# Layer 2's product from rows that are not yet normalized, and its end one half of the rows at a time beside layer 3's first sums

## Chip, core and metric

The kernel runs on one core of one Trainium2 chip. The metric is the time of one execution in device microseconds: the median of three runs of the kernel before is 1959.56 us (1958.17 to 1960.24). Durations below come from one profiled execution. The engines are PE (TensorE, with PEld for its weight loads), DVE (VectorE), ACT (ScalarE), POOL (GpSimd) and SP (SyncE, which issues most of the transfers).

## What is computed

Four graph layers run one after the other over N = 2708 nodes of D = 128 features with a weighted adjacency matrix of 2708 x 2708 (f32). After each layer its result is added to x and x is normalized over its features:

```python
x = _layernorm(x + layer0(x, adj, ...))   # layers 0 to 3 alike
# layer 0: messages gelu(s_i + d_j + b), weighted by adj, summed; update; gelu; + x; layernorm
# layer 1: messages = x @ W_msg + b; gates = sigmoid(q @ k.T / scale + bias) * adj * adj
#          relu([x, gates @ messages] @ W_upd + b); layernorm
# layer 2 (hyperbolic, curvature 1):
x = proj(x)
h = proj(mobius_matvec(W, x))             # tanh(|xW| / |x| * artanh|x|) * xW / |xW|
h = proj(mobius_add(h, proj(expmap0(b))))
local = logmap(h_i, h_j); att = sigmoid(scores) * adj
support = einsum('ij,ijd->id', att, local)
h = proj(expmap(support, h)); h = relu(logmap0(h)); return proj(expmap0(h))
# layer 3:
x1 = swish((adj @ x) @ W + b); x2 = swish((adj @ x1) @ W + b)
```

## The kernel before

The rows of x are 22 tiles of 128 (the last has 20 rows), in SBUF as x[128, 22, 128]. `runs()` (L190) splits them into two halves of 11 tiles, `groups()` into groups of four tiles. The compiler's scheduler orders the instructions, except inside `tc.manual_schedule()`, where they keep the order in which the program issues them. On each engine the instructions run in one fixed order. Transfers that SP issues go through its queue in that order.

*normalize* (L199) works out, from batch-norm statistics of 11 tiles, a scale r and an offset for each row: some ten short DVE operations and a Sqrt on ACT (L219). Then it applies them tile by tile, even tiles on DVE (L230), odd ones on ACT (L228).

*Resnorm* (L232) closes layers 0 and 1. `add` normalizes the layer's own output h, multiplies it by gamma, adds it to x and takes x's statistics (L238 to L243). `end` normalizes x. `all` does add for early rows, add for late rows, end for early, end for late. In layer 0, which is the function with the pair blocks, `U.norm.add(*early)` stands ahead of the last two groups' sums and rows (L885 to L893); a count `bad_n` of rows that the fast path can't handle follows (L896 to L907). Where it is above zero, the whole is computed again by other code, which didn't run here.

*Layer 1* (L976) first makes, group by group: four transposes of x, xT (copied by ACT, L1020), the message product mT (L1022, L1023), qT (L1026) and the rows of messages and updates (L1031, L1032), with w_both and b_both put together on POOL from four copies (L1000 and following). Then comes its loop over 22 adjacency tiles with the gates, in which `weights2` (L302 onward) makes layer 2's small weights step by step, one step per tile. It ends with `norm.all()`.

*Layer 2* starts with `transposed(xT, x)` (L1169, L259, L261), the products M = x W with three more columns (L1176, copied by ACT, L1177), statistics of M (L1179), and a long chain of 22-column operations to X. Then it transposes `prod[0]` and `prod[1]`, ten columns for each row tile, into `aux[0]` and `aux[1]`, and a score column into slB (L1250 to L1258). The pairs loop follows, up to about 1623 us.

*Layer 2's end* (`end(hf)`, L1443) takes one half of the rows through nine stages that are separated by `yield`: transposes of VT (L1475) into u and of V0T into V0; product and row sums (L1486, L1466); `each` (L1457), 11 instructions of one tile; squares on ACT (L1462); norms, tanh, artanh on 11 columns; `each` into x and its statistics (L1524, L1525); `normalize` (L1527). A loop (L1529 to L1536) lets the two halves take turns, stage by stage. Ahead of it SP loads VT0 and the first ten adjacency tiles, 1354 KB each, into `held`.

*Layer 3* (L1542) sums twice over the 22 tiles: `neighbours` issues for each tile six products of up to 512 columns (L1604, two passes each) into six PSUM banks, in a hand-written order of held (h) and streamed (f) tiles; three buffers stream the others. The last 3 (first pass) or 6 (second pass) tiles are taken bank by bank, and each bank's swish follows. All of this stands in a section of its own, whose pools open when layer 2's end has closed its own.

Of the kernel before, what the change touches and what calls it, by code (L numbers as in the profile page):

```python
# [39 lines left out]
def gnn_stack(ctx: ExitStack, tc: tile.TileContext, t, out: bass.AP):  # L40
# [32 lines left out]


    x = keep.tile([P, NT, D], F32, name="x")
    xsq = keep.tile([P, NT], F32, name="xsq")
# [24 lines left out]
    class Values:  # L101


        def __init__(self, pool, tag):
            self.pool, self.tag, self.n = pool, tag, 0
# [92 lines left out]

    def normalize(dst, src, st, a, b, V, sq=None):  # L199

# [20 lines left out]
        r = V.recip(V.add(root, V.mul(w, V.recip(root))))  # L221
        off = stt(both, -0.5, r, ALU.mult, ALU.mult)
        if sq is not None:
            nc.vector.scalar_tensor_tensor(sq[:, a:b], var, 4.0 * D, V.mul(r, r), op0=ALU.mult, op1=ALU.mult)
        for i in range(a, b):
            c = slice(i - a, i - a + 1)
            if i % 2:
                nc.scalar.activation(dst[:, i, :], src[:, i, :], AF.Identity, bias=off[:, c], scale=r[:, c])  # L228
            else:
                nc.vector.tensor_scalar(dst[:, i, :], src[:, i, :], r[:, c], off[:, c], op0=ALU.mult, op1=ALU.add)  # L230

    class Resnorm:  # L232


        def __init__(self, h, xb, g, st, st2, V, sq=None):
            self.h, self.xb, self.g, self.st, self.st2, self.V, self.sq = h, xb, g, st, st2, V, sq

        def add(self, a, b):  # L238
            h = self.h
            normalize(h, h, self.st, a, b, self.V)  # L240
            nc.vector.tensor_tensor(h[:, a:b, :], h[:, a:b, :], over_tiles(self.g, b - a), op=ALU.mult)
            nc.vector.tensor_tensor(x[:, a:b, :], self.xb[:, a:b, :], h[:, a:b, :], op=ALU.add)
            moments(self.st2, x, a, b)  # L243

        def end(self, a, b):
            normalize(x, x, self.st2, a, b, self.V, self.sq)

        def all(self):
            for a, b in runs():
                self.add(a, b)  # L250
            for a, b in runs():
                self.end(a, b)
# [49 lines left out]
    def weights2(pool, bank):  # L302
# [41 lines left out]
        nc.vector.tensor_copy(w2[:, D:], ps[:, :3])  # L344

# [31 lines left out]
    with ExitStack() as l0:  # L377
# [10 lines left out]
        with ExitStack() as msg:  # L388
# [449 lines left out]
            with tc.manual_schedule():  # L838
# [46 lines left out]
                early, late = runs()  # L885
                U.norm.add(*early)
                for n in range(ahead, G):
                    U.sums(n)
                for n in range(ahead, G):
                    U.rows(n)  # L890
                U.norm.add(*late)
                U.norm.end(*early)
                U.norm.end(*late)  # L893

# [10 lines left out]
                ps = p_misc.tile([P, BANK // P, P], F32, name="ps")  # L905
                nc.tensor.matmul(ps[:1, 0, :1], ones, most, start=True, stop=True)
                nc.vector.tensor_copy(bad_n, ps[:1, 0, :1])  # L907
# [68 lines left out]
    def layers_1_to_3(top, before_end=lambda: None):  # L976

        with ExitStack() as l1:
# [9 lines left out]
            w_both = wp.tile([P, 2 * D], F32, name="w_both")  # L988
            b_both = wp.tile([P, 2 * D], F32, name="b_both")
            xb = wp.tile([P, NT, D], F32, name="xb")  # L990
            w_msg, w_q, w_k = weight("L1_gnn_W_msg"), weight("L1_gnn_W_q"), weight("L1_gnn_W_k")
            upd_x, upd_a = weight("L1_gnn_W_upd", 0), weight("L1_gnn_W_upd", P)
            msg_bc, msg_br = column("L1_gnn_b_msg"), across("L1_gnn_b_msg")
            gate_b = across("L1_gnn_gate_bias")
            upd_b, gamma, beta = across("L1_gnn_b_upd"), across("L1_gnn_ln_gamma"), across("L1_gnn_ln_beta")

            with ExitStack() as pre:
                psum = pre.enter_context(tc.tile_pool(name="ps_pre1", bufs=2, space=PSUM))
                nc.gpsimd.memset(both[:, NT - 1, :], 0.0)
                for k, (w, b) in enumerate(((w_msg, msg_br), (upd_x, upd_b))):  # L1000
                    nc.gpsimd.tensor_copy(w_both[:, k * D:(k + 1) * D], w)
                    nc.gpsimd.tensor_copy(b_both[:, k * D:(k + 1) * D], b)
# [36 lines left out]
            with ExitStack() as att:  # L1039
# [8 lines left out]
                norm = Resnorm(h, xb, gamma, st, st2, Values(rp, "v1_"), xsq)  # L1048
# [40 lines left out]
                with tc.manual_schedule():  # L1089
# [25 lines left out]
                    norm.all()  # L1115
# [10 lines left out]
        with ExitStack() as l2:  # L1126
# [27 lines left out]
            with ExitStack() as pre:  # L1154
# [7 lines left out]
                prod = [pp.tile([P, NT, KP], F32, name=f"prod{k}") for k in range(2)]  # L1162
                part = [pp.tile([P, NT], BF16, name=f"part{q}") for q in range(3)]
                for k in range(2):
                    nc.gpsimd.memset(prod[k], 1.0)
# [28 lines left out]
                th = W.act(W.mul(W.mul(nM, s0), ax), AF.Tanh)  # L1194
# [55 lines left out]
                jobs = [(aux[k], KP, lambda i, r, k=k: prod[k][:r, i, :]) for k in range(2)]  # L1250
                jobs.append((slB, P, lambda i, r: sl[:r, i:i + 1].to_broadcast([r, P])))
                for dst, m, src in jobs:
                    for n, (a, b, r) in enumerate(groups()):
                        ps = psum.tile([P, BANK], F32, name="ps")
                        for i in range(a, b):
                            nc.tensor.transpose(ps[:m, (i - a) * P:(i - a) * P + r], src(i, r), ident[:r, :r])
                        w = (b - a - 1) * P + r
                        (nc.scalar.copy if n % 2 else nc.vector.tensor_copy)(dst[:, a * P:a * P + w], ps[:m, :w])  # L1258
# [162 lines left out]
        HELD = min(NT, 10)  # L1421
        held = top.enter_context(tc.tile_pool(name="adj3", bufs=1))
        kept = {}
# [4 lines left out]
        with ExitStack() as fin:  # L1428
            fp = fin.enter_context(tc.tile_pool(name="fin2", bufs=1))
            tp = fin.enter_context(tc.tile_pool(name="fin2t", bufs=2))  # L1430
            psum = fin.enter_context(tc.tile_pool(name="ps_fin2", bufs=6, space=PSUM))
            VT0 = fp.tile([P, HW], F32, name="VT0")
            nc.sync.dma_start(out=VT0, in_=v_tab)
            for j in range(HELD):
                kept[j] = held.tile([P, N], F32, name=f"held{j}")
                nc.sync.dma_start(out=kept[j], in_=adjT[j * P:(j + 1) * P, :])
            u = fp.tile([P, NT, D], F32, name="u")
            sv = fp.tile([P, NT, D], F32, name="sv")
            st = fp.tile([P, NT, 6], F32, name="st")
            nc.gpsimd.memset(u[:, NT - 1, :], 0.0)  # L1440
            nc.gpsimd.memset(V0, 0.0)

            def end(hf):  # L1443
                a, b = ((0, HT), (HT, NT))[hf]
                n = b - a
                V = Values(fp, f"v2{hf}_")
# [4 lines left out]
                def temp():  # L1451
                    return tp.tile([P, max(HT, NT - HT), D], F32, name="tmp")[:, :n, :]
# [36 lines left out]
                q = squares(uh)  # L1489
                yield  # L1490
# [38 lines left out]
            with tc.manual_schedule():  # L1529
                ends = [end(1), end(0)]  # L1530
                while ends:
                    for e in list(ends):
                        try:
                            next(e)
                        except StopIteration:
                            ends.remove(e)  # L1536
        xs.close()

        with ExitStack() as l3:  # L1542
            wp = l3.enter_context(tc.tile_pool(name="l3", bufs=1))
            STREAM = 3
            stream = l3.enter_context(tc.tile_pool(name="adj3s", bufs=STREAM))
            turns = l3.enter_context(tc.tile_pool(name="turns3", bufs=3))
            pacc = l3.enter_context(tc.tile_pool(name="ps_acc3", bufs=1, space=PSUM))
            psum = l3.enter_context(tc.tile_pool(name="ps_l3", bufs=2, space=PSUM))
            w3, b3 = weight("L3_gnn_W"), across("L3_gnn_b")
            V = Values(wp, "v3_")  # L1550
            nT = wp.tile([P, N], F32, name="nT")
            x1 = wp.tile([P, NT, D], F32, name="x1")
            st = wp.tile([P, NT, 6], F32, name="st")
            nc.vector.memset(x1[:, NT - 1, :], 0.0)
            banks = spans(0, N, BANK)

            def in_turns(pattern, near_by, far):

                near_by, far = list(near_by), list(far)
                order = [(near_by if c == "h" else far).pop(0) for c in pattern]  # L1560
                return order + near_by + far
# [27 lines left out]
            def neighbours(src, order, have, at_end, then, meanwhile=None):  # L1589
# [5 lines left out]
                def tile_of(j):  # L1595
                    at = have.get(j)
                    if at is None:
                        at = last[j] = stream.tile([P, N], F32, name="at")
                        nc.sync.dma_start(out=at[:rows[j], :], in_=adjT[j * P:j * P + rows[j], :])
                    return at  # L1600
# [6 lines left out]
                for j in order[:-at_end]:  # L1607
# [3 lines left out]
                    if meanwhile is not None and j == order[0]:  # L1611
                        meanwhile()
# [14 lines left out]
            def finish(a, b, r, g, gate):  # L1627
# [6 lines left out]
                normalize(x, x, st, a, b, V)  # L1634
# [7 lines left out]
            far = list(range(HELD, NT))[::-1]  # L1642
            near_by = list(range(HELD))
            last = {}
            with tc.manual_schedule():
                order = in_turns("hhfhfhfhfhffhffhfffhhf", near_by, far)
                first = neighbours(x, order, kept, 3, keep)
                back = far[::-1]
                have, last = kept | {j: last[j] for j in back[:STREAM]}, {}
                order = back[:STREAM] + in_turns("hfhfhfhffhfhhhhhfff", near_by, back[STREAM:])  # L1650

# [41 lines left out]
```

## Time and profile before

| what | us |
|---|---|
| median of three runs | 1959.56 |
| the profiled execution | 1961.88 |
| its span | 1960.2 |
| PE busy | 1662.2 (85%) |
| DVE busy | 1549.8 (79%) |
| ACT busy | 1119.8 (57%) |
| POOL busy | 676.7 (35%) |
| PE busy, 880 to 930 (layer 0's end) | 9.65 of 50 |
| PE busy, 960 to 1215 (layer 1's loop and end) | 222.11 of 255 |
| PE busy, 1631 to 1716 (layer 2's end) | 2.35 of 85 |
| PE busy, 1714 to 1822 (layer 3's first sums) | 107.96 of 108 |
| PE busy, 1822 to 1940 (layer 3's second sums) | 110.59 of 118 |

The page gives each engine's busy time, and then the span in 40 equal slices of 49 us, with one digit for the busy tenths of each. A group line has the source line, engine, operation, output and inputs with shapes and a count; then busy time and the mean of one in ns; then the idle time of the engine just before such an instruction and what ended most of it. A timeline line has start, duration, engine, line and operation, and in brackets the idle time before it and its releaser.

### The profile page before, as it was taken

To read this page: it belongs to the slowest core of one execution; us is meant where nothing else is said; L and a number is where in the kernel's file an instruction comes from. 1 tells how busy PE (TensorE), PEld (TensorE's weight loads), DVE (VectorE), ACT (ScalarE), POOL (GpSimd) and SP (SyncE) were. 2 spreads that over 40 slices of the span, in tenths; PEclk is the share of its full clock that TensorE was granted. 3 is DMA by queue.
4 is the path that set the end of the run, shared out by engine and by line. 5 is a ranking of instruction groups with operands and counts; after the bars stand their busy time and mean duration, and the time that the engine had idled before them with its cause. 6 is when DMAs were issued, how large, how long until landed. Compare 5 with 4: busy or idle time off the path is not lost.

```text
span 1960.2 us, 36493 instructions
## 1 busy us (share of the span) xinstructions
PE 1662.2 (85%) x13993; PEld 952.3 (49%) x13993; DVE 1549.8 (79%) x3657; ACT 1119.8 (57%) x1551; POOL 676.7 (35%) x431
## 2 busy tenths in 40 slices
PE   5999999999999999881999992889999972099995
PEld 5666666666666666661544442322223321044542
DVE  7899999999999999868588858699999997800104
ACT  3666676676666667553344434799989973300103
POOL 5667667767767767571100000020000440000000
PEclk8899999999999999995999996889989986589997
DMA  8756667667667666440344401122222207044320
GB/s 216 162 117 146 132 129 147 127 132 149 126 132 151 121 136 141 80 88 5 131 157 159 155 3 59 45 87 87 75 69 95 97 2 298 0 160 156 135 96 30
DMA packets 218695, 222.25 MB, mean 113 GB/s; under 512 B 28373, under 2 KB 204859, under 8 KB 212051
## 3 DMA queue, kind: packets, MB, share of 16 engines
q1 hardware_dynamic: 167470, 196.15, 32.8%
q0 software_dynamic: 51040, 23.68, 10.3%
q8 instruction: 111, 1.82, 0.4%
q14 instruction: 74, 0.60, 0.1%
HBM read 211.94 MB, written 7.83 MB: 112 GB/s over the span
## 4 chain that ended last, share of the span: by engine, by line
DVE 41%; PE 31%; POOL 9%; issue 7%; DMA 6%; ACT 6%; SPq 0%; DVEq 0%; ACTq 0%; POOLq 0%
PE acc L1604 10%; POOL far L739 8%; PE lg L1063 5%; PE acc L1070 5%; DVE ix L735 5%; DMA far<-d_tab,ix 3%; DVE W L840 3%; DVE u L1322 3%; DVE w L1336 3%; DVE m L1325 3%; DVE extra L753 2%; DVE o L697 2%; DVE m L1339 2%; DVE m L1342 2%; PE sl L775 2%
## 5 line engine op out<-in xcount | busy, mean ns | idle before, releaser
L739 POOL DMA_INDIRECT far<-d_tab,ix x352 | 561.7, 1596 | 260.1 <-DVE W L840 112.6
L853 ACT ACTIVATE g<-sl 128x768 f32<-128x768 f32 x484 | 393.4, 813 | 258.0 <-PE sl L780 201.9
L775 PE MATMUL sl<-dA,S 124*128 124x153 f16 x4840 | 408.9, 232 | 10.3 <-DVE W L840 7.8
L775 PEld LDWEIGHTS <-S 124*128 124x128 f16 x4840 | 331.1, 98 | 80.1 <-issue 68.4
L791 PE MATMUL acc<-g,W 128*32 128x128 f32 x4840 | 206.1, 278 | 0.5 <-DVE W L840 0.5
L1296 POOL TENSOR_TENSOR at<-at,off 128x128 f32<-128x128 f32 (+1 forms) x22 | 68.3, 3120 | 339.9 <-DVE m L1325 171.7
L791 PEld LDWEIGHTS acc<-g,W 128*32 128x32 f32 x4840 | 140.9, 109 | 58.8 <-issue 54.8
L1604 PE MATMUL acc<-held,x 128*128 128x512 f32 (+1 forms) x240 | 99.3, 562 | 82.6 <-ACT x L228 82.6
L780 PE MATMUL sl<-s,same 50*128 50x384 f16 x968 | 162.0, 308 | 0.0
L280 DVE TENSOR_TENSOR g<-ps,row_L_gnn_b 128x512 f32<-128x512 f32 (+2 forms) x14 | 7.9, 574 | 191.5 <-PE ps L278 191.5
L840 DVE TENSOR_TENSOR W<-sl,own 128x150 f32<-128x150 f32 x484 | 143.2, 300 | 14.9 <-ACT g L853 14.7
L1352 PE MATMUL accV<-m,X 128*128 128x512 f32 (+4 forms) x264 | 130.5, 637 | 27.4 <-DVE m L1342 26.5
L1304 PE MATMUL ps<-XT 128*128 128x512 f32 (+4 forms) x264 | 142.4, 622 | 6.4 <-DVE m L1307 3.3
L1064 ACT ACTIVATE w<-lg,row_L_gnn_gate_bias 128x512 f32<-128x512 f32 (+1 forms) x132 | 83.5, 636 | 106.1 <-PE lg L1063 104.8
L665 DVE TENSOR_SCALAR S<-rk 124x1000 f16<-124x1000 bf16 (+1 forms) x330 | 133.2, 429 | 0.0
L735 DVE FIND_INDEX8 ix<-v,o 128x8 uint32<-128x2728 f32 x44 | 131.7, 2994 | 0.0
L1063 PE MATMUL lg<-qT,mT 128*128 128x512 f32 (+2 forms) x264 | 121.2, 547 | 3.6 <-ACT w L1064 3.1
L1070 PE MATMUL acc<-w,both 128*128 128x512 f32 (+2 forms) x264 | 121.2, 547 | 0.0
L753 DVE SCALAR_TENSOR_TENSOR extra<-far,v,extra 128x128 f32<-128x128 f32 x330 | 114.9, 348 | 6.3
L1604 PE MATMUL acc<-at,x 128*128 128x512 f32 (+3 forms) x288 | 118.4, 559 | 0.0
L697 DVE SCALAR_TENSOR_TENSOR o<-ps,ar 128x496 f32<-128x496 f32 x132 | 82.5, 625 | 37.5 <-issue 22.6
L1604 PEld LDWEIGHTS acc<-held,x 128*128 128x128 f32 x240 | 45.0, 196 | 134.8 <-ACT x L228 82.9
(315 smaller groups left out, 2634.8 us busy)
## 6 DMA issues: line engine op xcount, KB each, us to landing
at<-in_adjT SPq DMA_DIRECT2D x40, 1354.0 KB
ar<-in_adj SPq DMA_DIRECT2D x105, 248.0 KB
far<-s_tab SPq DMA_DIRECT2D x44, 512.0 KB
at<-in_adjT SPq DMA_DIRECT2D x42, 448.0 KB
at<-in_adjT SPq DMA_DIRECT2D x21, 704.0 KB
at<-in_adjT SPq DMA_DIRECT2D x21, 650.0 KB
held<-in_adjT SPq DMA_DIRECT2D x10, 1354.0 KB
at<-in_adjT SPq DMA_DIRECT2D x21, 280.0 KB
```

The costliest lines, as they stand in the source:

```text
L735: nc.vector.max_index(ix, self.v[:, n * 8:n * 8 + 8], self.o.rearrange("p b j -> p (b j)"))
L739: nc.gpsimd.indirect_dma_start(out=self.far[n][:, k, :], out_offset=None, in_=d_tab[:, :], in_offset=bass.IndirectOffsetOnAxis(ap=self.ix[ ...
L753: nc.vector.scalar_tensor_tensor(self.extra, f, w, self.extra, op0=ALU.mult, op1=ALU.add)
L775: nc.tensor.matmul(group[c], self.S[h][:, n, c, :], dA[q][:, b, c, :], start=c % 3 == 0 and q == 0, stop=False)
L780: nc.tensor.matmul(out, same[p], self.s3[p, :e - a, :], start=False, stop=True)
L791: nc.tensor.matmul(self.acc[q:q + 32, k, :], W[:, c, :], g[:, c, :], start=b == 0 and k == 0, stop=ends)
L840: nc.vector.tensor_tensor(W[:, :, :RG].rearrange("p (k c) i -> p k c i", k=2), columns_of(sl, D, DA), own[:, None, None, :].to_broadcast([ ...
L853: nc.scalar.activation(g.rearrange("p (k c) d -> p k c d", k=2), columns_of(sl, 0, D), AF.Gelu, scale=1.0 / D_SCALE)
L1063: nc.tensor.matmul(lg, mT[:, j * P:j * P + r], qT[:, a:b], start=True, stop=True)
L1070: nc.tensor.matmul(acc[k], mrow[:rows[j], j, :], ws[j][:rows[j], a:b], start=j == 0, stop=j == NT - 1)
L1304: nc.tensor.matmul(ps, XT[:, self.js], XT[:, c], start=True, stop=False)
L1604: nc.tensor.matmul(acc[k], src[:rows[j], j, :], at[:rows[j], a:b], start=j == order[0], stop=j == order[-1])
```

## The change

1. `normalize` is split into `normalizer` (statistics to scale and offset) and `shift` (apply them, with a string that says which engine takes which tile). `Resnorm.begin` is the first half of the old `add`, with all shifts on ACT; `add` goes in groups of four tiles.
2. Layer 0: the count of bad rows first, then early rows begun and added, the last two groups' sums and rows between, late rows begun, early rows ended with all shifts on DVE, late rows added and ended.
3. Layer 1: w_both and b_both are loaded side by side. Its end is `all_but_end`: both halves begun, both added, and one normalizer over 22 columns gives scale xr, offset xo and xsq. x itself stays unnormalized.
4. Layer 2's product takes these rows with W's columns centred (one more step in `weights2`), and xr enters the norm of x. Its end applies the shift to x, a half at a time, on ACT between two of its stages.
5. The two aux sets are transposed together, 42 columns, and copied by ACT (first) and DVE (second).
6. Layer 2's end and layer 3 share one section. Half 1 goes through `end` completely, then half 0. Layer 3's first pass takes half 1's 11 tiles first (21, 11, 20, 12, 19, 13, 18, 14, 17, 15, 16), then half 0's (0, 10, 9, 2, 8, 7, 3, 6, 5, 1, 4). Held are tiles 11 to 15, 0 and 1. Tiles 2 and 3 are loaded into X's space and into the space of VT0 and the temporaries, when half 0's end has used them. The PSUM pool for the transposes has two buffers (six before), the pool for the swish two (three before).

```diff
+    def shift(dst, src, a, b, by, turns="va"):
+        r, off = by
         for i in range(a, b):
             c = slice(i - a, i - a + 1)
-            if i % 2:
+            if turns[i % len(turns)] == "a":
                 nc.scalar.activation(dst[:, i, :], src[:, i, :], AF.Identity, bias=off[:, c], scale=r[:, c])
             else:
                 nc.vector.tensor_scalar(dst[:, i, :], src[:, i, :], r[:, c], off[:, c], op0=ALU.mult, op1=ALU.add)
...
+        def begin(self, a, b):
+            shift(self.h, self.h, a, b, normalizer(self.st, a, b, self.V), "a")
         def add(self, a, b):
-            h = self.h
-            normalize(h, h, self.st, a, b, self.V)
-            nc.vector.tensor_tensor(h[:, a:b, :], h[:, a:b, :], over_tiles(self.g, b - a), op=ALU.mult)
-            nc.vector.tensor_tensor(x[:, a:b, :], self.xb[:, a:b, :], h[:, a:b, :], op=ALU.add)
-            moments(self.st2, x, a, b)
+            for k, m in spans(a, b, 4):
+                h = self.h[:, k:m, :]
+                nc.vector.tensor_tensor(h, h, over_tiles(self.g, m - k), op=ALU.mult)
+                nc.vector.tensor_tensor(x[:, k:m, :], self.xb[:, k:m, :], h, op=ALU.add)
+                moments(self.st2, x, k, m)
+        def end(self, a, b, turns="va"):
+            shift(x, x, a, b, normalizer(self.st2, a, b, self.V), turns)
+        def all(self, between=lambda: None):
+            early, late = runs()
+            self.begin(*early)
+            self.add(*early)
+            between()
+            self.begin(*late)
+            self.end(*early, "v")
+            self.add(*late)
+            self.end(*late)
+        def all_but_end(self):
+            for a, b in runs():
+                self.begin(a, b)
+            for a, b in runs():
+                self.add(a, b)
+            normalizer(self.st2, 0, NT, self.V, xsq, (xr, xo))
...
         nc.vector.tensor_copy(w2[:, D:], ps[:, :3])
+        yield
+        ps = bank()
+        nc.vector.tensor_scalar(w_rows, ident, -1.0 / D, None, op0=ALU.add)
+        nc.tensor.matmul(ps[:, :D + 3], w_rows, w2, start=True, stop=True)
+        nc.vector.tensor_copy(w2, ps[:, :D + 3])
...
-                th = W.act(W.mul(W.mul(nM, s0), ax), AF.Tanh)
+                th = W.act(W.mul(W.mul(nM, W.mul(s0, xr)), ax), AF.Tanh)
...
+                for n, c, ps in turned(lambda i, r: prods[:r, i, :], 32 + KP):
+                    nc.scalar.copy(aux[0][:, c], ps[:KP])
+                    nc.vector.tensor_copy(aux[1][:, c], ps[32:32 + KP])
...
+        HELD, STREAM = 7, 3
+        near1 = list(range(HT, HT + 5))
+        near0 = list(range(HELD - len(near1)))
+        spare0 = list(range(len(near0), len(near0) + 2))
+        far1 = [j for j in range(HT, NT) if j not in near1][::-1]
+        far0 = list(range(spare0[-1] + 1, HT))[::-1]
...
+            x1, nT = u, sv.rearrange("p n d -> p (n d)")[:, :N]
...
                 q = squares(uh)
+                shift(x, x, a, b, (xr[:, own], xo[:, own]), "a")
                 yield
...
-                ends = [end(1), end(0)]
-                while ends:
-                    for e in list(ends):
-                        try:
-                            next(e)
-                        except StopIteration:
-                            ends.remove(e)
...
+                ends = [end(1), end(0)]
+                for e in ends:
+                    next(e)
+                for e in ends:
+                    for _ in e:
+                        pass
+                def more():
+                    for j, at in spare.items():
+                        kept[j] = fetch(j, at)
+                order = (in_turns("fhfhfhfhfhf", h=near1, f=far1)
+                         + in_turns("hffsffsffhf", h=near0, f=far0, s=spare0))
+                first = neighbours(x, order, kept, 3, keep, more, len(far1 + near1) - 1)
+                back = (far1 + far0)[::-1]
                 have, last = kept | {j: last[j] for j in back[:STREAM]}, {}
-                order = back[:STREAM] + in_turns("hfhfhfhffhfhhhhhfff", near_by, back[STREAM:])
+                order = back[:STREAM] + in_turns("hfhfhfhffhffhhhhfff", h=kept, f=back[STREAM:])
```

## The prediction, before the result was known

> **What bounds the kernel now.** I read first the page's slices, then the windows around the one long hole in TensorE's row, the waits and the timeline there, and last the two smaller holes.
>
> ```profile
> PE   5999999999999999881999992889999972099995
> ...
> L1604 PE MATMUL acc<-held,x 128*128 128x512 f32 (+1 forms) x240 | 99.3, 562 | 82.6 <-ACT x L228 82.6
> ```
>
> PE is full nearly everywhere, so time can be won only in the slices that read 0 to 2: slice 35 (about 1666 to 1715 us), slice 19 (about 880 to 930) and slice 25 (about 1176 to 1225). The largest is before layer 3's first sums (L1604): a single wait of 82.6 us for a normalized x.
>
> ```profile
> 1631.00:1656.00 25.00, 0.39 (x4) 0.15 (x2) 22.28 (x67) 9.42 (x12) 0.00 (x0) 0.61 1.00 425
> 1656.00:1716.00 60.00, 1.96 (x3) 0.96 (x4) 52.27 (x221) 22.01 (x31) 0.00 (x0) 0.50 0.05 22
> 1740.00:1800.00 60.00, 60.00 (x159) 28.37 (x159) 0.00 (x0) 0.00 (x0) 0.00 (x0) 1.00 0.48 171
> ```
>
> Columns: window, length, busy PE, PEld, DVE, ACT, POOL, PE clock, DMA share, GB/s. While PE stands still, DVE is busy 74.6 of 85 us with the two halves of layer 2's end, turn by turn. Once layer 3 runs, PE is busy 60.00 of 60 us and DVE 0.00. So DVE's 85 us and PE's first sums lie one after the other, though each half of x feeds half of the tiles. By 1656 the adjacency tiles are in SBUF: DMA isn't the limit.
>
> ```profile
> 1635.43 2.98 DVE L1457 SCALAR_TENSOR_TENSOR u<-X,v,u 128x128 f32<-128x128 f32 x11
> 1646.58 1.28 ACT L145 ACT_TABLE_LOAD   x1
> 1709.75 2.42 ACT L228 ACTIVATE x<-x,v,v 128x128 f32<-128x128 f32 x6 [1.17 <-DVE v L205]
> 1738.11 4.71 PE L1604 MATMUL acc<-at,x 128*128 128x512 f32 x12
> ```
>
> These are the prices: 2.98 us for 11 row tiles on DVE, 1.28 for a table, 0.40 a tile for ACT's shift, and about 4.71 us a tile on PE (12 instructions, two passes for each of six banks).
>
> **What the Trainium skill says.** "TensorE: Matmul & The Clock Gate", What you observe: matmuls run at about half speed until some 4 us of sustained activity. The trace agrees: from 1714.04 the products are 0.85 us apart, after 1718.3 0.43. "ScalarE: Activation LUTs", What ACT_TABLE_LOAD costs: 1283 ns, and about 1380 ns of drain more. The trace has 1.28 us, but the Sqrt begins 0.02 us after the load (1646.58 + 1.28, then 1647.88), so I charge 1.3 and no drain. "DMA: Bandwidth & Descriptors", Where 436 GB/s comes from: the ports end at about 435; here 425.
>
> **Part 1, layer 2's end half by half.** Both halves' transposes stay first, with two PSUM buffers instead of six: each of the eight groups may wait for its copy (4 tiles, about 0.5 us on ACT). Zero to 3 us; I take 0.9. Then half 1 goes alone through the chain that in the trace both shared. Step by step, from 1631.65, the end of V0's copies:
> - product and sum 1.62 + 1.62, small steps 0.5, eleven tiles 2.98: u at 1638.4; square 1.38 on ACT: 1639.9.
> - New here: normalizing x, left out of layer 1, stands on ACT between the square and the Sqrt. Eleven shifts at 0.39: 4.35, to 1644.25. Table 1.3, Sqrt 0.2: 1645.75. In the meantime DVE's sum (1.62) is done, so about 3.9 of the 4.35 lie on this half's chain.
> - reciprocal and products to the tanh 1647.3; eleven tiles 1650.6; square and sum 1653.7; small steps 0.95; eleven tiles 1657.6; two squares on ACT 1660.5; second sum 1662.4; Sqrt 1663.1, small steps 1664.1.
> - artanh and tanh, in the trace 1684.68 to 1689.85: 5.2, to 1669.2; tanh, reciprocals 1.3: 1670.5; eleven tiles 1673.5; statistics 2.15: 1675.7.
> - normalizer 2.07 (1707.68 to 1709.75): 1677.75; six shifts on ACT 2.42: 1680.2.
>
> With 0.9 for the transposes PE can start at about 1681.1 instead of 1714.04: a gain of 33. In the new order tile 21 comes first, and its x is the last of those six shifts, so no earlier start is possible. Half 1 has 11 tiles at 4.71 = 51.8 and about 3 for the slow clock at the start, as now: to about 1736. Half 0 begins on DVE at about 1679 (DVE's queue has it behind half 1) and needs the same 48: ready at about 1727, 9 us before PE asks. So it is hidden entirely, and the rest of layer 3 keeps its length and moves by 33. If that cover went, each us of half 0 beyond 9 would cost one us.
>
> What is moved and queued: SP fetches seven held and three streamed tiles (ten, as now), then tile 2 into X and tile 3 into the room of VT0 and the temporaries. These two wait on DVE's last use, about 1705 and 1711, and the remaining seven are queued behind them. The first of those is asked for at about 1741, 30 us later, and a tile takes 3.3 us at 425 GB/s: no wait. The second pass streams ten tiles instead of nine; before its last group of six tiles the last fetch has one tile and some of the next (about 8 us) to land in instead of about 12: 0, at worst 2. Range of the part: 26 (transposes 3, stages 2, a second slow clock 2) to 36 (shift half hidden, no PSUM wait, fewer small gaps).
>
> **Part 2, layer 1's end and layer 2's product.** Before, layer 1's additions end at 1196.7; then both halves are normalized, transposed and multiplied, and the statistics of M end at 1212.63.
>
> ```profile
> 1192.88 1.62 DVE L242 TENSOR_TENSOR x<-xb,both 128x1408 f32<-128x1408 f32 x1
> 1208.87 3.76 DVE L1179 BATCH_NORM_STATS2 st<-M 128x6 f32<-128x128 f32 x19
> 1236.46 4.23 PE L1256 MATMUL ps<-ident,prod 128*10 128x128 f32 x22 [0.71 <-DVE prod L1237]
> ```
>
> After: late rows' Sqrt waits on ACT behind eleven early shifts (1179.1 to 1183.5), and DVE waits for it until 1183.7, with all additions queued behind. Then 1.1, then six groups: mult, add and statistics of four tiles 2.25, of three 1.8, in all 12.6: 1197.4, no gain so far. But transposes and products of the earlier groups run beside that. Left on DVE after 1197.4: memset 0.91 and mask 0.22, one normalizer of 22 columns about 2.6, four xT copies at 0.69 = 2.8, 22 statistics at 0.2 = 4.4: 10.7, to 1208.1. Gain 4.5; the extra product with the rows' scale is 0.2. Bounds 2 (PE or the copies of M late) and 7 (copies before the additions end).
>
> The aux transposes: 44 of ten columns in 7.45 us (1236.46 to 1243.9) become 22 of 42. One set takes about 0.19 x 22 = 4.2, but each group is copied twice (ACT 0.57, then DVE 0.68, three buffers), so about 4.5 to 5.5 instead of 7.45, and the vector that slB needs is not held up by DVE's copies. Gain 3 (1 to 5). Together 7.5, bounds 3 and 12. Centring W is one tensor_scalar, one matmul of 128x131 and one copy, a further step inside layer 1's loop: 0.3 + 0.4 + 0.4 on engines that are busy there 206 (DVE) and 222 (PE) of 255 us, about 0.7 lost, 0 to 1.5.
>
> **Part 3, layer 0's end.** Before: early additions end 909.3, late 921.5, early rows normalized 925.1, late 929.6; then layer 1's first transposes, and PE needs about 4.3 us for each group of four tiles; the third group's message product starts at 943.46. After: early shifts on ACT alone (11 x 0.39) with additions in groups, to about 910.5; sums 5 and 6 and late statistics to 915.7; late shifts 4.3 on ACT, early rows' Sqrt behind them: 920.2. DVE's eleven early shifts 3.0: 924.4, so PE gets the first tiles at about 922.5 instead of 931.5. But two groups only. Late additions (6.3) lie on DVE between layer 1's copies (six, 4.1): to about 935; their Sqrt is on ACT behind the first two groups' work, and late rows are there from about 938.4; 2 us for transposes and copy, and the third group's product starts at 940.5 to 941. Gain 2.5, bounds 0 (late rows as late as 941.5) and 6 (PE never waits). The bias and weight copies on POOL that fall away lay beside DVE: 0.
>
> **Sum.** 33 + 7.5 - 0.7 + 2.5 = 42.3. The profiled execution took 1961.88 with a span of 1960.2; it becomes 1919.6 with a span of 1917.9. The median of the runs shown is 1959.56, 2.3 below: 1917.3.
>
> **Rivals.**
> - **The chain for half 1 is longer than I add up** (two PSUM buffers, DVE alone exposing each hand-over to ACT that the other half now fills): PE at about 1694, gain 20 instead of 33, 29.3 in all: 1930. For it: the waits list DVE for ACT only 5.3 us in six times, because the halves fill each other's gaps; against it: I took the steps from unshared stretches. Half 0 would be longer too, and past 9 us PE would wait a second time.
> - **More is won** (both front stages near their upper bounds, 12 and 6, and 36 in the end): 54, 1905.6. For it: PE starts sooner after its last work in three places.
> - **No overlap, slower:** the first product waits for the later end as well. Two ends one after the other put PE's start at 1680.2 + 0.9 + 47.5 = 1728.6, 14.5 after 1714.04; the front stages give 9.3 back: 5.2 slower, 1964.8. It decides as soon as half 0's chain ends ahead of PE's first product; with the given order, it would take a wait on ACT or on a shared buffer that covers both. Against it: in the changed order of instructions the first product waits for ACT's shift of tile 21, issued before half 0's steps. This is also the case in which the change doesn't do what it says.
>
> **How the numbers follow.** Likeliest 0.61: 1917.3 (its own range 1907 to 1930 from the bounds above, not all reached together). Longer chain 0.20: 1930. More won 0.13: 1905.6. No overlap 0.04: 1964.8. Other, near no change, 0.02. The range 1905 to 1931 leaves out about 2 in 10. About 0.2% (3.9 us) is what a measurement can tell from no change: faster 0.95, within 0.015, slower 0.035.
>
> **What would show it.** The first L1604 product at about 1671 (1681 less the 9.3 of the front), DVE busy some 48 us beside PE after it, PE without a hole between the halves; statistics of M about 7 earlier, first logits of layer 1 about 2.5 earlier. It is wrong if PE stops before tile 0, if SP's fetch of tile 2 or 3 holds up tile 10, or if the first product waits for half 0.

## The result, and the profile after

| | before | after |
|---|---|---|
| median, us | 1959.60 (4 runs) | 1919.07 (4 runs, 1918.73 to 1919.40) |
| ratio, 95% interval | | 0.9788 (0.9776 to 0.9800) |
| profiled execution, us | 1961.88 | 1919.40 |
| its span, us | 1960.2 | 1917.7 |

The forecast was 1917.3 (1905 to 1931). The kernel is 40.5 us faster by the medians of all runs, 42.5 by the spans of the two profiled executions. The slices of the page of after, and its group of layer 3's products:

```profile
PE   5899999999999999885699996689998996199995
...
L1634 PE MATMUL acc<-at,x 128*128 128x512 f32 (+2 forms) x156 | 66.2, 574 | 48.8 <-ACT x L246 48.8
```

One slice still reads below 5 (the 1); before, four read 0 to 2, two of them (2 and 0) in this hole. The wait before layer 3's first product is 48.8 us instead of 82.6. Three windows of after: half 1's end alone, layer 3's first tiles, and the middle of the second sums (columns as in the prediction).

```profile
1624.00:1672.00 48.00, 0.00 (x0) 0.00 (x0) 38.19 (x142) 20.77 (x33) 0.00 (x0) 0.52 0.53 215
1672.00:1729.00 57.00, 56.65 (x129) 25.94 (x130) 37.03 (x141) 19.50 (x32) 0.00 (x0) 0.87 0.44 171
...
1790.00:1870.00 80.00, 80.00 (x215) 37.47 (x214) 2.60 (x7) 1.83 (x4) 0.00 (x0) 1.00 0.43 159
```

In the second window PE is busy 56.65 of 57 us and DVE 37.03: half 0's end lies beside the sums of half 1, as meant. PE's clock there is 0.87 on average, and the timeline says where it is low:

```profile
1672.35 9.36 PE L1634 MATMUL acc<-at,x 20*128 20x512 f32 x12 [48.83 <-ACT x L246]
1681.64 7.41 PE L1634 MATMUL acc<-held,x 128*128 128x512 f32 x12
1688.89 4.71 PE L1634 MATMUL acc<-at,x 128*128 128x512 f32 x12
...
1725.23 4.71 PE L1634 MATMUL acc<-at,x 128*128 128x512 f32 x12
1729.78 4.71 PE L1634 MATMUL acc<-held,x 128*128 128x512 f32 x12
```

The first tile, of 20 rows, takes 9.36 us instead of 4.71, the next 7.41. The tile at 1729.78 is tile 0, the first that needs half 0, and PE goes over to it without a pause. Half 0's last shift is this line on ACT, done at 1717.5, 12.3 us earlier:

```profile
1715.45 2.03 ACT L246 ACTIVATE x<-x,VT 128x128 f32<-128x128 f32 x5 [1.17 <-DVE VT L235]
```

To see where the 42.5 us come from, I cut both traces at the starts of the same events: the last four-tile group of statistics in layer 0, layer 1's first logits, its last update product, the last statistics of M, the first product of layer 2's end, the first of layer 3, and the end.

| stage | before | after | difference | forecast |
|---|---|---|---|---|
| layer 0, to its last four-tile statistics | 897.0 | 895.6 | -1.4 | 0 |
| to the first logits | 61.6 | 59.7 | -1.9 | -2.5 |
| layer 1's loop, to the last update product | 216.3 | 218.4 | +2.1 | +0.7 |
| to the last statistics of M | 37.5 | 32.7 | -4.8 | -4.5 |
| aux, pairs and transposes, to layer 2's end | 419.3 | 417.4 | -1.9 | -3 + 0.9 |
| half 1's end, to layer 3's first product | 82.3 | 48.6 | -33.7 | -33.9 |
| layer 3 | 246.2 | 245.3 | -0.9 | 0 |

### The profile page after: what moved, and what is told of

It is laid out like the page before. It is cut to its first block, busy times and chain, and to the rows that moved or that the text cites. A ratio compares the mean times of both kernels' runs of the same rounds, so it can differ in the third digit from the quotient of the medians.

```text
span 1917.7 us, 36464 instructions
## 1 busy us (share of the span) xinstructions
PE 1659.6 (87%) x13973; PEld 949.3 (50%) x13973; DVE 1542.7 (80%) x3632; ACT 1132.0 (59%) x1581; POOL 680.1 (35%) x426
## 4 chain that ended last, share of the span: by engine, by line
DVE 37%; PE 32%; POOL 10%; issue 7%; ACT 7%; DMA 6%; SPq 0%; DVEq 0%; ACTq 0%; POOLq 0%
PE acc L1634 10%; POOL far L781 9%; PE lg L1098 5%; PE acc L1105 5%; DVE ix L777 5%; DMA far<-d_tab,ix 3%; DVE w L1375 3%; DVE u L1361 3%; DVE m L1364 3%; DVE W L882 3%; PE sl L817 2%; DVE extra L795 2%; DVE m L1381 2%; DVE o L739 2%; DVE m L1378 2%
## 5 line engine op out<-in xcount | busy, mean ns | idle before, releaser
L1634 PE MATMUL acc<-at,x 128*128 128x512 f32 (+2 forms) x156 | 66.2, 574 | 48.8 <-ACT x L246 48.8
L1100 DVE TENSOR_TENSOR w<-w,at 128x512 f32<-128x512 f32 (+1 forms) x132 | 82.5, 625 | 27.2 <-ACT w L1099 27.1
L1391 PEld LDWEIGHTS accV<-m,X 128*128 128x128 f32 (+1 forms) x264 | 52.1, 211 | 97.0 <-issue 57.7
```

The lines of the kernel that those rows point to most:

```text
L1391: nc.tensor.matmul(accV[:, a:b], X[:self.r, self.j, :], self.m[:, a:b], start=first, stop=last)
L1634: nc.tensor.matmul(acc[k], src[:rows[j], j, :], at[:rows[j], a:b], start=j == order[0], stop=j == order[-1])
```

## Experiments

The theory was that nearly all of the gain is the overlap in layer 2's end, and that the front stages give a few us each. The rivals: the gain comes from opening layer 3's pools and loading ahead; parts 2 and 3 are worth nothing, or cost something. All times stand beside runs of the kernel before on the same chip (medians 1961.53 for e1 to e4, 1960.72 for e0 and e5 to e7, 1961.36 for e8 to e11), so the ratios compare best. The stages of the profiled runs, cut as above, in us (the first is given where it is spoken of):

| kernel | to logits | layer 1's loop | to M's statistics | to layer 2's end | to layer 3 | layer 3 | ratio, 95% interval |
|---|---|---|---|---|---|---|---|
| e0, after again | 60.4 | 218.4 | 32.9 | 417.5 | 48.5 | 245.3 | 0.9779 (0.9766 to 0.9791) |
| e3, shift later | | 218.4 | 32.8 | 417.6 | 44.8 | 245.3 | 0.9773 (0.9759 to 0.9786) |
| e4, last tile late | | 218.4 | 32.8 | 417.5 | 47.4 | 245.7 | 0.9776 (0.9763 to 0.9790) |
| e5, centre early | | 216.8 | 32.0 | 416.7 | 48.5 | 245.1 | 0.9777 (0.9764 to 0.9789) |
| e6, normalized product | | 216.2 | 37.2 | 414.6 | 44.5 | 244.0 | 0.9757 (0.9744 to 0.9770) |
| e7, aux apart | | 218.4 | 32.6 | 420.6 | 48.2 | 245.2 | 0.9810 (0.9797 to 0.9822) |
| e8, layer 0 as before | 56.0 | 218.4 | 33.0 | 417.6 | 48.2 | 245.5 | 0.9760 (0.9744 to 0.9776) |
| e9, e3 and e5 | 59.7 | 216.8 | 31.9 | 415.8 | 44.8 | 245.5 | 0.9756 (0.9742 to 0.9769) |
| e10, e9 and e4 | | 216.7 | 32.0 | 415.8 | 43.8 | 241.7 | 0.9729 (0.9716 to 0.9743) |
| e11, e6 and e4 | | 216.3 | 37.2 | 414.6 | 43.5 | 241.7 | 0.9737 (0.9724 to 0.9751) |

**e0.** The changed kernel unaltered.

> The changed kernel itself, as the measure for the kernels beside it on the same chip. Every theory expects its ratio of 0.9788 to the kernel before again, within 0.0012.

Median 1918.12, in the expected range. Its five runs go from 1916.06 to 1920.81, so 2 us between two kernels are read from the stages of the traces rather than from medians. A stage whose code is unchanged repeats within 0.2 us in e3, e4 and e8, but not always: the stage to the first logits takes 58.9 us in e7 and 59.7 to 60.4 in the other kernels in which it is the same.

**e1. Tile 0 first: no overlap.**

```diff
                          + in_turns("hffsffsffhf", h=near0, f=far0, s=spare0))
+                order.insert(0, order.pop(order.index(0)))
```

> The changed kernel, with tile 0 (half 0) moved to the front of the first pass, so that layer 3's first product waits for both ends in turn. Theory (the gain in layer 3 is the overlap): the first product comes when half 0's x is ready, 45.2 us later than now (1717.5 against 1672.35 in the profile of after), less about 1.8 because a full tile now comes ahead of the 20-row tile: 1919.1 + 43.4 = 1962.5, so no faster than the kernel before. Rival (the gain came from opening layer 3's pools early and from fetching ahead, not from the overlap): not above 1935.

Median 1960.12, ratio 0.9993 (0.9984 to 1.0001). With one tile moved in PE's order the whole gain is gone, although the pools, the fetches and the serial ends are as in the changed kernel. The timeline of e1:

```profile
1716.82 7.33 PE L1634 MATMUL acc<-held,x 128*128 128x512 f32 x12 [92.38 <-DVE x L248]
1724.08 4.81 PE L1634 MATMUL acc<-at,x 20*128 20x512 f32 x12
1728.81 6.47 PE L1634 MATMUL acc<-held,x 128*128 128x512 f32 x12
```

PE waits 92.4 us. This is the prediction's third rival, made real, and by the ratios (0.9993 less 0.9788) it costs 40 us, for which I had 43.4: counted from the first product of layer 2's end, layer 3 starts 43.5 us later (92.06 for 48.5), and layer 3, which now begins with a full tile, is 3.1 shorter (242.2 for 245.3). e1 is level with the kernel before, where that rival had 5.2 slower. The rival about the pools falls.

**e2. The halves take turns again.** (Half 0 has two temporaries of its own.)

```diff
...
-                for e in ends:
-                    for _ in e:
-                        pass
+                while ends:
+                    for e in list(ends):
+                        try:
+                            next(e)
+                        except StopIteration:
+                            ends.remove(e)
```

> The changed kernel with the two halves of layer 2's end taking turns stage by stage again, half 0 with two temporaries of its own. Theory (the halves done one after the other give the overlap): half 1's x comes 80.5 us after its first product as in the trace of before (1631.72 to 1712.17) or up to 5 later because of the added shifts, so at 1704 to 1709 instead of 1672.35: 32 to 37 us slower, 1951 to 1956. Rival (half 1 ahead in layer 3's order is enough, whichever way the ends are interleaved): under 1935.

Median 1953.22, in the expected range, ratio 0.9956 (0.9941 to 0.9971). The first product in e2:

```profile
1705.99 9.36 PE L1636 MATMUL acc<-at,x 20*128 20x512 f32 x12 [82.60 <-ACT VT L156]
```

So half 1 first in PE's order is worth little as long as DVE works at both halves in turn. It is the serial ends and the order of tiles together that give the 33 us.

**e3. The shift two stages later.**

```diff
                 q = squares(uh)
-                shift(x, x, a, b, (xr[:, own], xo[:, own]), "a")
                 yield
...
                 q = squares(svh)
+                shift(x, x, a, b, (xr[:, own], xo[:, own]), "a")
```

> The changed kernel with the eleven shifts of x moved two stages later on ACT, behind the square of sv, where ACT otherwise waits 5.66 us for DVE. Theory (about 3.9 of the 4.32 us lie on half 1's chain): 3.9 faster, 1915.2. Rival (DVE alone sets the chain, ACT's shifts lie beside it): 1919 within 0.7.

Median 1917.07. In the trace the stage of half 1's end falls from 48.5 to 44.8, as expected: 3.7. ACT's timeline in e3:

```profile
1639.94 1.38 ACT L1518 ACTIVATE room<-sv 128x1408 f32<-128x1408 f32 x1 [3.59 <-DVE sv L1513]
1641.23 4.32 ACT L246 ACTIVATE x<-x,xo,xr 128x128 f32<-128x128 f32 x11
1646.98 1.38 ACT L1518 ACTIVATE room<-sv 128x1408 f32<-128x1408 f32 x1 [1.43 <-DVE sv L1513]
```

Behind the shifts ACT still waits 1.43 us for DVE, so here they cost nothing. By the ratios alone the gain would be 1.2 us relative to e0, within both intervals. e9 below, with the same edit, has 44.8 again.

**e4. The 20-row tile in the last group.** Tile 21 is held, and taken bank by bank with the last tiles of both passes.

```diff
-        near1 = list(range(HT, HT + 5))
+        near1 = list(range(HT, HT + 4)) + [NT - 1]
...
-                order = (in_turns("fhfhfhfhfhf", h=near1, f=far1)
-                         + in_turns("hffsffsffhf", h=near0, f=far0, s=spare0))
+                order = (in_turns("fhfhfhfhff", h=near1[:-1], f=far1)
+                         + in_turns("hffsffsfflhf", h=near0, f=far0, s=spare0, l=near1[-1:]))
...
```

> The changed kernel with the 20-row tile 21 held and taken in the bank-by-bank group at the end of both passes, so that layer 3 begins with full tiles. Theory (a product of 20 rows doesn't bring the PE clock up: 12 products at 0.78 us, and then the usual 4.3 us at half speed): the slow start costs 2.1 instead of 7.35 us, 5.2 faster: 1913.9. Rival (the clock needs some 14 us after so long a pause whatever runs): 1919 within 1.

Median 1918.42: the expected 5.2 us don't show. The timeline of e4 has the expected start, and then something else near the end:

```profile
1672.05 7.44 PE L1634 MATMUL acc<-at,x 128*128 128x512 f32 x12 [47.78 <-DVE x L248]
1679.33 4.71 PE L1634 MATMUL acc<-held,x 128*128 128x512 f32 x12
...
1879.48 2.08 PE L314 MATMUL ps<-w_L_gnn_W,sv 128*128 128x128 f32 x8 [2.67 <-ACT sv L1603]
1881.35 4.87 PE L1634 MATMUL acc<-at,u 128*128 128x512 f32 x6
```

The start costs one slow tile (7.44) where it was 9.36 and 7.41, so the rival of some 14 us whatever runs falls; the first two tiles of the pass take 11.8 us instead of 16.5. The first product also comes 1.0 us earlier (47.4 for 48.5), since it no longer waits for ACT's last shift, that of tile 21. But after a pause of 2.67 us in the last pass the clock was low again: 4.87 us for six products. In e10, with the same order, the same place reads

```profile
1871.46 1.16 PE L314 MATMUL ps<-w_L_gnn_W,sv 128*128 128x128 f32 x8 [2.68 <-ACT sv L1604]
1872.45 2.74 PE L1635 MATMUL acc<-at,u 128*128 128x512 f32 x6
```

after a pause as long. The products of these two lines make 3.0 of the 4.0 us by which layer 3 is longer in e4 than in e10. The order has a price of its own too: e11 saves 4.7 us on the first two tiles against e6, which has the other order (10.7 for 15.4), but only 2.3 in layer 3 (241.7 for 244.0). So the edit is worth some 2.3 us in layer 3 and 1.0 ahead of it. e10 gains 3.8 in layer 3 against e9, but in e9 too the pause was followed by slow products (4.58 us for six that take 2.93 in after), which cost it 1.65. Whether such a pause is followed by a low clock differs from one execution to the next, and between before and after too:

```profile
1922.30 1.44 PE L278 MATMUL ps<-w_L_gnn_W,nT 128*128 128x128 f32 x8 [2.48 <-ACT nT L1571]
1923.53 4.38 PE L1604 MATMUL acc<-at,x 128*128 128x512 f32 x6
...
1882.16 1.16 PE L314 MATMUL ps<-w_L_gnn_W,sv 128*128 128x128 f32 x8 [2.48 <-ACT sv L1603]
1883.16 2.93 PE L1634 MATMUL acc<-at,u 128*128 128x512 f32 x6
```

The first two lines are of before, the others of after. That this explains all five runs of e4 isn't shown.

**e5. The centring matrix early.**

```diff
+        centre = pool.tile([P, D], F32, name="y2_centre")
+        nc.vector.tensor_scalar(centre, ident, -1.0 / D, None, op0=ALU.add)
...
-        nc.vector.tensor_scalar(w_rows, ident, -1.0 / D, None, op0=ALU.add)
-        nc.tensor.matmul(ps[:, :D + 3], w_rows, w2, start=True, stop=True)
+        nc.tensor.matmul(ps[:, :D + 3], centre, w2, start=True, stop=True)
```

> The changed kernel with the centring matrix (identity less 1/128) made once at the start of the small-weights steps, in a tile of its own, so that the centring product in layer 1's loop waits for nothing new on DVE. Theory (of the 2.1 us that layer 1's loop lost, 1.67 are PE's wait for that DVE operation behind the gates' products): 1.7 faster than the changed kernel. Rival (the loop's loss is the product's own 0.46 us and chance): 0 to 0.4 faster.

Layer 1's loop falls from 218.4 to 216.8. What it removes is this wait in the trace of after, in which DVE's 0.22 us come behind the gates' products in its queue:

```profile
1053.12 0.22 DVE L384 TENSOR_SCALAR y_w_rows<-ident 128x128 f32<-128x128 f32 x1
1053.48 0.46 PE L385 MATMUL lg<-w,y_w_rows 128*128 128x131 f32 x2 [1.67 <-DVE y_w_rows L384]
```

The median is 1917.25, 0.9 below e0: right by the stage, too small for the medians. In the same trace the two stages behind the loop are 0.9 and 0.8 shorter, for which the edit gives no reason that I can see, so a stage of a single trace can be off by about 1 us.

**e6. The product from normalized rows.** Part 2 without its aux half: layer 1 ends as before, W isn't centred, layer 2's end has no shift.

```diff
             for a, b in runs():
-                self.begin(a, b)
-            for a, b in runs():
-                self.add(a, b)
-            normalizer(self.st2, 0, NT, self.V, xsq, (xr, xo))
+                normalize(h, h, self.st, a, b, self.V)
...
+            for a, b in runs():
+                normalize(x, x, self.st2, a, b, self.V, xsq)
...
-                th = W.act(W.mul(W.mul(nM, W.mul(s0, xr)), ax), AF.Tanh)
+                th = W.act(W.mul(W.mul(nM, s0), ax), AF.Tanh)
...
```

> The changed kernel with part 2's first half undone: layer 1's end normalizes x again, half by half, as before, layer 2's product takes normalized rows with W not centred, and layer 2's end applies no shift. Theory (the pieces of the ledger: 4.7 won up to M's statistics, but 2.1 lost in layer 1's loop and about 3.9 on half 1's chain for the shift): 1.3 faster than the changed kernel. Rival (rows that are not yet normalized are a gain in all, since the shift is hidden): 2.6 to 4.7 slower.

Median 1913.81, 4.3 below e0: the raw product, as the change makes it, is a loss. The stages say how: +4.3 up to M's statistics (37.2 for 32.9), but -2.2 in the loop, -4.0 in half 1's end. A further -2.9 between M's statistics and layer 2's end and -1.3 in layer 3 I hadn't expected; one short product of 22 columns accounts for some 0.2. Most of both isn't due to the raw rows: e9, which has them too, takes 415.8 us in that stage, against 417.5 in e0, and in layer 3 its second tile takes 6.17 us and that of e6 6.31, where e0 has 7.41. Without these, the stages put the loss at some 3 us rather than 6.

**e7. The aux sets apart.** The two sets of 22 transposes are back as in the kernel before.

```diff
-                prods = pp.tile([P, NT, 32 + KP], F32, name="prods")
-                prod = [prods[:, :, k:k + KP] for k in (0, 32)]
+                prod = [pp.tile([P, NT, KP], F32, name=f"prod{k}") for k in range(2)]
...
+                jobs = [(aux[k], KP, lambda i, r, k=k: prod[k][:r, i, :]) for k in range(2)]
...
```

> The changed kernel with the two aux sets transposed one after the other again, 44 transposes of ten columns. Theory (by the marks of the two traces the joint set is worth 7.1 less 5.9, since PE takes pair products between its groups and each group is copied twice): 1.2 slower. The prediction's own term: 3 slower. Rival (nothing, the score vector for slB comes no earlier): 0 within 0.5.

Ratio 0.9810, against 0.9779 for e0: 6 us by the ratios, 3.1 in the stage to layer 2's end (420.6 for 417.5). (One of its six executions took 5296 us, for which no run shows a cause; the ratio is of the other five.) The sign is clear: the fastest of e7, 1921.56, lies above the slowest of e0, 1920.81. The size isn't. Of the 3.1, 0.85 lie behind the last pair product (9.14 us from there to layer 2's end, 8.29 in e0), and e5, which has the joint set, takes 9.13 there. So the prediction's term of 3 is compatible with the runs, which put it at 2 to 6 us; my 1.2 is below that.

**e8. Layer 0's end as before.**

```diff
-            self.begin(*early)
-            self.add(*early)
-            between()
-            self.begin(*late)
-            self.end(*early, "v")
-            self.add(*late)
-            self.end(*late)
+            h = self.h
+            for n, (a, b) in enumerate(runs()):
+                if n:
+                    between()
+                normalize(h, h, self.st, a, b, self.V)
...
+            for a, b in runs():
+                self.end(a, b)
```

> The changed kernel with layer 0's end in the order and split of the kernel before (early rows added, the last sums, late rows added, early ended, late ended, shifts on DVE and ACT in turn). Theory (the order of part 3 brings the first logits 1.9 earlier, measured between the ends of layer 0's statistics and the logits in the two traces): 1.9 slower than the changed kernel. Prediction's term: 2.5 slower. Rival (the 3.3 us by which the logits came earlier are chance of layer 0's long loop): 0 to 0.5 slower.

The opposite came out: median 1914.8, ratio 0.9760, and the stage takes 56.0 us instead of 60.4. The part that e8 keeps is the count of bad rows, whose work on DVE stands ahead of the halves and whose product on PE between them. PE's timeline in the kernel before:

```profile
929.67 0.19 PE L906 MATMUL ps<-most,ones 128*1 128x1 f32 x2 [33.03 <-DVE most L904]
930.10 0.48 PE L1007 MATMUL ps<-ident,w_L_gnn_W_q 128*128 128x128 f32 x1 [0.24 <-DVE bad_n L907]
...
931.76 1.91 PE L1019 MATMUL ps<-ident,x 128*128 128x128 f32 x8
```

and in e8:

```profile
909.34 0.80 PE L1049 MATMUL ps<-wT,wT 128*128 128x128 f32 x2 [0.38 <-DVE wT L1046]
923.34 1.94 PE L1056 MATMUL ps<-ident,x 128*128 128x128 f32 x8 [13.21 <-DVE x L248]
```

Before, the transposes of x stood in PE's queue behind a product of 0.19 us, which counts bad rows and waited for DVE's last work. With the count out of the way they start as soon as the first early tiles are there, and the stage is 5.6 shorter than before (61.6 to 56.0). e8 keeps the side-by-side loads of w_both and b_both too, but they can't be the cause: from the transposes to the first logits PE takes 26.9 us before (931.76 to 958.61) and 27.1 in e8 (923.34 to 950.40), so all of the gain lies ahead of them. The new order of the halves gives 3.7 to 4.4 of the 5.6 back (2.9 in e7), since it makes the late half, which the third group needs, later. In after PE begins the transposes at 920.46, but then waits for tile 11:

```profile
935.40 1.37 PE L1054 MATMUL ps<-ident,x 128*128 128x128 f32 x5 [3.67 <-DVE x L248]
937.91 2.08 PE L1057 MATMUL ps_m<-xT,w_both 128*128 128x512 f32 x2 [1.14 <-ACT xT L1055]
```

Behind these waits PE's clock is low (0.57 on average from 936 to 944 us): the two products of L1057 take 2.08 us together, the same two 1.12 in e8 and 1.13 before. From there to the first logits it is 17.4 us, against 15.1 in e8 and before.

**e9. Shift later and centre early; e10. the last tile late besides; e11. e6 with the last tile late.**

> The changed kernel with both mendings: the shift of x two stages later, and the centring matrix made early. Theory (the two lie in different stages, so they add up): 3.8 + 1.6 = 5.4 faster than the changed kernel, about 1912.7 where that takes 1918.1; then the product from raw rows is a small gain over normalized rows (1913.8). Rival (each of them only moves a wait): under 3 faster.

> The kernel e9 and, besides, the 20-row tile in the bank-by-bank groups. Theory (in the trace of e4 the first pass gains 2.8 us and the end of the second loses it again through PE pauses of 2.7 us, after which it runs at half speed): 0 to 3 faster than e9. Rival (the start alone counts): 5 faster than e9.

> The kernel e6 (product from normalized rows, no shift, no centring) and, besides, the 20-row tile in the bank-by-bank groups. Theory: 0 to 3 faster than e6, so 1911 to 1914, about the same as e10. Rival (raw rows are needed for the gain): 3 or more slower than e10.

Medians 1913.15, 1908.58 and 1909.93. e3 and e5 add up: 1913.15 for 1912.7 expected. With the two mendings the raw product is no loss any more: e9 is level with e6 (1913.15 and 1913.81). e10 is 4.6 below e9, more than the 0 to 3 that I gave it after e4 and nearer its rival's 5. e10 and e11 can't be told apart by their ratios, whose intervals overlap; the stages from the first logits on add up to 950.0 us in e10 and 953.3 in e11, which would be a small gain of the raw product. e10, at 0.9729, beats both kernels. e10 with layer 0's end from e8 was not run; if the 4.4 us between e8's and e0's stages added up with it, it would take about 1904.

## Why the prediction was right, step by step

*The chain of half 1.* Forecast 48.5 us from the end of V0's copies, measured 48.6 from the first product. The stages were summed from stretches of the trace in which the two halves didn't share an engine. Laid on the trace of after, with the first products set to the same time, the marks of the list are met within 0.3 us (u at 1638.5, the shifts done at 1644.1, the last six shifts at 1680.1), so no hand-over between DVE and ACT cost more alone than shared. The first rival, the longer chain, is refuted by this stage alone.

*The shift on the chain.* "about 3.9 of the 4.35 lie on this half's chain": e3 took 3.7 away.

*The cover for half 0.* Forecast 9 us to spare, measured 12.3. The slow start of PE is longer than I had put (16.77 us for the first two tiles, so 7.4 lost instead of about 3), which lengthens the cover. Most of it had stood in the trace of before: 5.5 lost there, on the first two tiles and then around the 20-row tile. I had taken the start to cost the same as before; it costs 1.9 more. That layer 3 came out 0.9 shorter all the same is luck in the main: the slow products behind the pause of 2.48 us shown under e4 cost 1.7 us before and nothing in after; another 1 us is open.

*Fetches.* No wait of PE between the first tile and tile 0, nor around the tiles fetched into X and the room.

*PSUM buffers.* Forecast +0.9. Aux, pairs and transposes together were forecast at -2.1 and gave -1.9; the two buffers alone weren't tried. The stretch from the last pair product to layer 2's end took 9.05 us before, 8.29 in after and 7.2 to 9.1 in other kernels with two buffers, so its own scatter hides a term of this size.

*Part 2.* "Gain 4.5" up to M's statistics: 4.8. (The terms left on DVE add up to 10.9, not the 10.7 of the text, which makes it 4.3.) Aux 3: right in sign by e7, its size between 2 and 6. The centring was mis-sized: "about 0.7 lost, 0 to 1.5" became 2.1, outside my bounds. I had counted its busy times and not that PE waits for a DVE operation queued behind the gates. Nobody is idle there, so the 1.67 us are lost in full.

*Part 3.* "Gain 2.5", measured 1.9, but by another mechanism. I credited the order of the halves. e8 shows that this order costs some 4 us, and that moving the count ahead, to which I gave no price at all, gains 5.6. This step was wrong, and that its sum came near is luck.

*The sum.* 42.3 forecast, 42.5 by the spans, 40.5 by the medians. The agreement is better than the terms deserve: the loop and layer 0 were off by 1.4 each way. Layer 0's own 1.4 us lie within what executions of the same instructions differ by (that mark is at 895.6 in after, 896.2 in e0 and 894.4 in e8).

## What to carry to other kernels

When one engine works through a long serial stage for two halves while the next stage's engine stands still, let it finish one half first, and give the next engine that half's work; neither the order of the consumer nor that of the producer does it alone. Of each moved step ask what stands behind it in the queue of the engine that it waits on: a product of 0.19 us at the head of PE's queue was worth 5.6 us here, and an operation of 0.22 us on DVE cost 1.67. Test the parts of a change singly even if the sum is as forecast: two parts of this one cost some 3 to 4 us each as they were built.

## What the runs showed of the hardware

A tile of 20 rows didn't bring PE's clock up. In after, behind the long pause, its twelve products ran at 0.78 us each from first to last (9.36), and the next full tile still had some 5 us at half speed (clock 0.50 up to 1686.8, 1.00 from 1687.2). With that order this next tile took 6.17 (e9) to 7.58 us (e7, e8). A full tile at the start reached full speed within itself: 6.24 us in e10, 6.33 in e11, 7.33 in e1 and 7.44 in e4, and then 4.71 or 4.81. In e1 a 20-row tile behind a full one still ran at full speed (4.81), and the tile after it was slow (6.47). The Trainium skill's "TensorE: Matmul & The Clock Gate" (What you observe) has some 4 us of sustained activity up to full speed; it is only with full tiles that these traces come near that figure (an estimate from those tiles: 1.5 to 2.7 us lost at half speed are 3 to 5.5 us of it).

The pause in the last pass, 2.48 to 2.68 us long, was followed by slow products in three of the fourteen profiled executions (before and e9, 2.48; e4, 2.67) and by products at full speed in the other eleven. The next pause there, 4.30 to 4.50 us, was followed by slow products in all fourteen (2.07 or 2.08 us for the eight of L314 or its counterpart). The same page (HAM oscillation) names some 3.4 us as the pause to stay under; the three slow cases are shorter than that.
